# A graph attention layer's rank order and block lists through scatters to memory, and two broadcast rows through transfers

## Chip, cores and metric

One core of one Trainium2 chip. The metric is the device time of one launch in microseconds (us), of which medians are quoted. Ratios are formed only within one submission; where profiles or times of different submissions are set side by side, the text says so. In the profile's lines and in the recorded texts PE is TensorE, DVE is VectorE, ACT is ScalarE, POOL is GpSimd, and SP is the engine whose queue asks for the panels of `adj`; L173 is line 173 of the kernel.

## The reference, cut to what matters

Four graph layers run over the same dense 2708 x 2708 matrix `adj` with 128 features. The change touches layer 1 alone, a graph attention:

```python
XW = X @ W
s_col, s_row = XW @ a[:f], XW @ a[f:]              # called c and r in the kernel
den = exp(leaky_relu(s_row[:, None] + s_col[None, :], 0.01))
num = A @ den
att = where(num != 0, den / num, 0)
H = A @ (att @ XW)
```

The kernel avoids forming `den` densely. It ranks the nodes by c, sorts rows of XW by rank, assigns every node i to one of NB = 43 blocks of ranks (where -r_i falls among the sorted c), and gets `num` from one dense pass (`lc` against all of adj) plus, for each block, a small correction over the at most 128 nodes listed for it. The pass goes through six chunks of columns, four of them 512 wide, by 22 tiles of rows; 16 of these tiles are loaded for each chunk as four panels, the rest stay on the core. These are 132 matmuls in the program. The trace shows each as two records, and the "264 matmuls" of the prediction are records.

Of the kernel before, what the change touches and what calls it, by code (L numbers as in the profile page):

```python
# [8 lines left out]
F32 = mybir.dt.float32  # L9
U32 = mybir.dt.uint32  # L10
I32 = mybir.dt.int32
BF16 = mybir.dt.bfloat16
AF = mybir.ActivationFunctionType
ALU = mybir.AluOpType
AX = mybir.AxisListType

P = 128
# [4 lines left out]
KC = 126  # L22
OOB = 4095
# [27 lines left out]
def kernel(  # L51
# [16 lines left out]
    nc = tc.nc  # L68
    N, D = x.shape
    assert D == P  # L70
    T = (N + P - 1) // P
# [6 lines left out]
    FULL = N // P  # L78
    LAST = N - FULL * P
    NQ = T  # L80
    S = T - RES
    NB = (N + BJ - 1) // BJ
    HALF = N // 2
    pw = [min(P, N - t * P) for t in range(T)]
# [6 lines left out]
    big = ctx.enter_context(tc.tile_pool(name="big", bufs=1))  # L91
# [5 lines left out]
    dram = ctx.enter_context(tc.tile_pool(name="dram", bufs=1, space=bass.MemoryType.DRAM))  # L97
# [4 lines left out]
    def mis_tile():  # L102
        return mis_pool.tile([P, CW], F32, tag="mis", name="mis")
# [19 lines left out]
    ident = const.tile([P, P], F32, tag="ident", name="ident")  # L123
# [18 lines left out]
    def evacuate(n, dst, src):  # L142
        if n % 2:
            nc.scalar.copy(dst, src)
        else:
            nc.vector.tensor_copy(dst, src)
# [70 lines left out]
                op0=ALU.subtract, op1=ALU.mult,  # L217
            )

    def rows_from(dst, col, ts, exp_scale=None):  # L220

        ts = list(ts)
        for g in range(0, len(ts), 4):
            grp = ts[g : g + 4]
            ps = mis_tile()
            w = 0
            for t in grp:
                nc.tensor.transpose(
                    ps[:, w : w + pw[t]], col[: pw[t], t : t + 1].to_broadcast([pw[t], P]), ident[: pw[t], : pw[t]]
                )  # L230
                w += pw[t]
            if exp_scale is None:
                evacuate(g // 4, dst[:, g * P : g * P + w], ps[:, :w])
            else:
                nc.scalar.activation(dst[:, g * P : g * P + w], ps[:, :w], AF.Exp, scale=exp_scale)

    def linear(t, wgt):

        po = mis_tile()
# [11 lines left out]
    e_r = att1.tile([P, T], F32, tag="e_r", name="e_r")  # L251
    f_r = att1.tile([P, T], F32, tag="f_r", name="f_r")
    f_out = att1.tile([P, T], F32, tag="f_out", name="f_out")
    jidx = att1.tile([P, NQ], U32, tag="jidx", name="jidx")
    csort = att1.tile([P, NQ], F32, tag="csort", name="csort")
    g_col = att1.tile([P, NQ], F32, tag="g_col", name="g_col")
    g_inv = att1.tile([P, NQ], F32, tag="g_inv", name="g_inv")
# [299 lines left out]


    wide = ctx.enter_context(tc.tile_pool(name="wide", bufs=1))
    xwe = wide.tile([P, T, D + 1], F32, tag="wide", name="xwe")  # L560
    late = ExitStack()
    got_pool = late.enter_context(tc.tile_pool(name="got", bufs=16))
    sum_pool = late.enter_context(tc.tile_pool(name="sum", bufs=1))
# [31 lines left out]



    xw_rows = dram.tile([N, D], F32, tag="xw_rows", name="xw_rows")
    if LAST:
        nc.gpsimd.memset(xwe[:, FULL, :], 0.0)  # L600
        nc.gpsimd.memset(cc[:, FULL:], 0.0)
# [46 lines left out]
    def times_w(c, t):  # L648
        p, o = pw[t], t * P - starts[c]
        po = mis_tile()  # L650
        nc.tensor.matmul(po[:p, : D + 1], lhsT=xTs[c][:, o : o + p], rhs=wae[:, : D + 1], start=True, stop=True)
        nc.scalar.copy(xwe[:p, t, :], po[:p, : D + 1])

    def compare(t):
        p, o = pw[t], t * P
# [57 lines left out]
        due.flush()  # L713
    late.close()
    lwx = ctx.enter_context(tc.tile_pool(name="lwx", bufs=1))
    xws = lwx.tile([P, NQ, D], F32, tag="xws", name="xws")
    lw = lwx.tile([P, NB, BJ], F32, tag="lw", name="lw")
    g_row = hT

    with tc.tile_pool(name="rank", bufs=1) as rank, tc.tile_pool(name="rank2", bufs=2) as rank2:  # L720
        def rtile(shape, name, dt=F32):
            return rank.tile([P] + shape, dt, tag=name, name=name)

        nc.scalar.dma_start(xw_rows[: FULL * P, :].rearrange("(t p) d -> p t d", p=P), xwe[:, :FULL, :D])
        if LAST:
            nc.scalar.dma_start(xw_rows[FULL * P :, :], xwe[:LAST, FULL, :D])
        nc.vector.tensor_copy(rr, xwe[:, :, D])
        nc.scalar.activation(e_r, rr, AF.Exp)
        nc.scalar.activation(f_r, rr, AF.Exp, scale=0.01)

        rk_f = rtile([T], "rk_f")
        nc.vector.memset(rk_f, float(OOB))
# [2 lines left out]
        nc.vector.tensor_add(rk_f[:, : T - 1], after[:, : T - 1], rows_m[:, : T - 1])  # L735
        lp = pw[T - 1]
        nc.vector.tensor_add(rk_f[:lp, T - 1 :], after[:lp, T - 1 :], rows_m[:lp, T - 1 :])


        grid = [P, T, NB]  # L740
# [46 lines left out]
        nc.vector.tensor_scalar_mul(f_out, f_out, -1.0)  # L787

        place = rtile([T, NB], "place")
        totals = rtile([T, NB], "totals")  # L790
        for t0, t1 in halves:
            rhs = in_b[:, t0:t1, :].rearrange("p t b -> p (t b)")
            for dst, lhs in ((totals, ones_b), (place, upper_b)):
# [10 lines left out]
        nc.vector.tensor_reduce(pos, place, AX.X, ALU.add)  # L804


        val_b = big.tile([P, T, 3, NB], F32, tag="y", name="val_b")
        for n, v in enumerate((node_oob, e_r, f_r)):
            nc.vector.tensor_mul(val_b[:, :, n, :], in_b, v[:, :, None].to_broadcast(grid))
        sl = mis_tile()  # L810
        for t in range(T):
            at = rank2.tile([P, P], F32, tag="at", name="at")
            nc.vector.tensor_scalar(at, iota, pos[:, t : t + 1], None, op0=ALU.is_equal)
            nc.tensor.matmul(
                sl[:, : 3 * NB], lhsT=at, rhs=val_b[:, t, :, :].rearrange("p a b -> p (a b)"),
                start=(t == 0), stop=(t == T - 1),
            )
        for h in range(2):
            nc.vector.tensor_scalar(
                slot_i[h], sl[:, :NB], 2.0, 2.0 * OOB + h, op0=ALU.mult, op1=ALU.add  # L820
            )

        nc.vector.tensor_scalar_add(slot_e, sl[:, NB : 2 * NB], ident[:, KC : KC + 1])
        nc.vector.tensor_scalar_add(slot_f, sl[:, 2 * NB : 3 * NB], ident[:, KC + 1 : KC + 2])


        rk_i = rtile([T], "rk_i", I32)
        nc.vector.tensor_copy(rk_i, rk_f)
        hi_i = rtile([T], "hi_i", I32)
        nc.vector.tensor_single_scalar(hi_i, rk_i, 7, op=ALU.arith_shift_right)  # L830
        hi = rtile([T], "hi")
        nc.vector.tensor_copy(hi, hi_i)
        lo = rtile([T], "lo")
        nc.vector.scalar_tensor_tensor(lo, hi, -float(P), rk_f, op0=ALU.mult, op1=ALU.add)
        of_q = rtile([T, NQ], "of_q")
        nc.vector.tensor_tensor(
            of_q, hi[:, :, None].to_broadcast([P, T, NQ]), iota[:, None, :NQ].to_broadcast([P, T, NQ]),
            op=ALU.is_equal,
        )
        val_q = big.tile([P, T, 2, NQ], F32, tag="y", name="val_q")  # L840
        nc.vector.tensor_mul(val_q[:, :, 0, :], of_q, node[:, :, None].to_broadcast([P, T, NQ]))
        nc.vector.tensor_mul(val_q[:, :, 1, :], of_q, cc[:, :, None].to_broadcast([P, T, NQ]))
        js = mis_tile()
        for t in range(T):
            at = rank2.tile([P, P], F32, tag="at", name="at")
            nc.vector.tensor_scalar(at, iota, lo[:, t : t + 1], None, op0=ALU.is_equal)
            nc.tensor.matmul(
                js[:, : 2 * NQ], lhsT=at, rhs=val_q[:, t, :, :].rearrange("p a q -> p (a q)"),
                start=(t == 0), stop=(t == T - 1),
            )  # L850
        nc.vector.tensor_copy(jidx, js[:, :NQ])
        nc.vector.tensor_copy(csort, js[:, NQ : 2 * NQ])
        nc.scalar.activation(g_col, csort, AF.Exp, scale=0.99)
        nc.scalar.activation(g_inv, csort, AF.Exp, scale=-0.99)
        for q in range(NQ):
            p = pw[q]
            nc.gpsimd.indirect_dma_start(
                out=xws[:p, q, :], out_offset=None, in_=xw_rows[:, :],
                in_offset=bass.IndirectOffsetOnAxis(ap=jidx[:p, q : q + 1], axis=0),
                bounds_check=N - 1, oob_is_err=False,  # L860
            )
            nc.scalar.mul(xws[:p, q, :], xws[:p, q, :], g_col[:p, q : q + 1])
        rows_from(g_row, csort, range(T), 0.99)
        for b in range(NB):
            nc.vector.tensor_scalar(
                lw[:, b, : bw[b]], g_row[:, b * BJ : b * BJ + bw[b]], slot_e[:, b : b + 1], slot_f[:, b : b + 1],
                op0=ALU.mult, op1=ALU.max,
            )

    gb = hT  # L870
    rows_from(gb, rr, range(T), 0.99)
    carry = big.tile([P, N], F32, tag="y", name="carry")

    def mix(w, q, num, col, haccs, pool):

        p = pw[q]
        inv = pool.tile([P, w], F32, tag=f"inv{w}", name="inv")
        nc.scalar.activation(inv[:p], num[:p, :w], AF.Ln)  # L878
        nc.scalar.activation(inv[:p], inv[:p], AF.Exp, scale=-1.0)  # L879

        err = pool.tile([P, w], F32, tag=f"err{w}", name="err")
        nc.vector.tensor_mul(err[:p], inv[:p], num[:p, :w])  # L882
        nc.vector.scalar_tensor_tensor(err[:p], err[:p], 2.0, inv[:p], op0=ALU.subtract, op1=ALU.mult)  # L883
        nc.vector.scalar_tensor_tensor(  # L884
            err[:p], gb[:p, col : col + w], g_inv[:p, q : q + 1], err[:p], op0=ALU.max, op1=ALU.mult
        )
        for o in range(0, w, CW):
            e = min(w, o + CW)
            nc.tensor.matmul(  # L889
                haccs[:, o:e], lhsT=xws[:p, q, :], rhs=err[:p, o:e], start=(q == 0), stop=(q == NQ - 1)  # L890
            )

    def end_carry(c, acc):
# [179 lines left out]
```

## The kernel before: the parts that the change touches

`xwe` holds XW and r; it and `lc` are tiles of one pool with a single buffer.

```python
wide = ctx.enter_context(tc.tile_pool(name="wide", bufs=1))
xwe = wide.tile([P, T, D + 1], F32, tag="wide", name="xwe")
# ... ranks counted (rk_f), blocks found ...
nc.scalar.dma_start(xw_rows[: FULL * P, :].rearrange("(t p) d -> p t d", p=P), xwe[:, :FULL, :D])
lc = wide.tile([P, T, NB, 2], F32, tag="wide", name="lc")   # same buffer as xwe

# block lists: a one-hot compare on VectorE and a matmul on TensorE per tile of nodes
for t in range(T):
    nc.vector.tensor_scalar(at, iota, pos[:, t : t + 1], None, op0=ALU.is_equal)
    nc.tensor.matmul(sl[:, : 3 * NB], lhsT=at, rhs=val_b[:, t, :, :].rearrange("p a b -> p (a b)"),
                     start=(t == 0), stop=(t == T - 1))
# order of ranks: the same with lo/hi of the rank and val_q, giving jidx and csort
# ... cut ...
for q in range(NQ):                        # rows of XW by rank: 22 gathers, each then scaled
    nc.gpsimd.indirect_dma_start(out=xws[:p, q, :], in_=xw_rows[:, :], in_offset=...jidx[:p, q : q + 1]...)
    nc.scalar.mul(xws[:p, q, :], xws[:p, q, :], g_col[:p, q : q + 1])
rows_from(g_row, csort, range(T), 0.99)    # e^.99c on all partitions: 22 turns on TensorE, Exp on ScalarE
rows_from(gb, rr, range(T), 0.99)          # e^.99r: 22 more
carry = big.tile([P, N], F32, tag="y", name="carry")
by_panels(lambda i: lc[: pw[i], i, :, :]..., end_carry)     # the dense pass: 264 records
```

A scheduler orders the instructions of each engine, so the turns and one-hot matmuls above stand inside the pass in TensorE's order. "Turn" means a transpose by a matmul with the identity.

## Time and profile before

| kernel before | us |
|---|---|
| timed, first submission, median of 3 | 1162.3 (1160.76 to 1163.44) |
| the profiled execution | 1204.79 (span 1203.1) |
| last rank count on TensorE ends | 483.05 |
| pass of layer 1 | 490.35 to 634.53 |
| from the ranks to the end of the pass | 151.5 |

The last row is the measure used below: it contains what the change moves up to the end of the pass. What follows the pass took 568.4 to 576.4 us in the 13 profiles (568.6 here, 573.3 in the first profile of the changed kernel and 568.4 in the second), in no order by kernel; differences of some us in the total can lie there. Note at once that the profiled execution is 3.7% slower than the timed ones; what that means becomes clear only in the experiments. The profile's own lines stand in the prediction.

### The profile page before, as it was taken

What the parts mean: (1) busy time and instruction counts of PE and PEld (TensorE: products, weight loads), DVE (VectorE), ACT (ScalarE), POOL (GpSimd) and SP (SyncE); (2) the same over time, 40 slices, a digit from 0 to 9 for tenths busy, and PEclk for the clock granted to TensorE, in tenths of its full rate; (3) what the DMA queues carried; (4) which work ended last, traced back from release to release, by engine and by line L of the source; (5) the groups of instructions that cost most, each with busy time, mean ns of one, the idle gap of its engine ahead of it and who ended that gap; (6) DMA issues with size and microseconds to landing.
All of it is one profiled execution on the core that took longest, in us unless ns stands there. A gap on an engine that the chain in (4) does not pass through costs nothing. (4 is left out here: it accounts for less than half of the span.)

```text
span 1203.1 us, 11015 instructions
## 1 busy us (share of the span) xinstructions
PE 1088.8 (91%) x3625; PEld 515.5 (43%) x3625; DVE 657.8 (55%) x1428; ACT 317.5 (26%) x591; POOL 264.9 (22%) x261
## 2 busy tenths in 40 slices
PE   1899999999946995796799999999899999999997
PEld 1355444443423473253243333333344554465445
DVE  6875469999215476843005999999712112123122
ACT  0001145554001245104005566666311010002000
POOL 4000000001574670007014555565001000000000
PEclk9899999999977896798799999999899999999999
DMA  9994410002715461541653453455375675664754
GB/s 351 372 296 170 141 35 0 1 1 89 269 48 173 150 205 41 176 147 46 202 159 117 149 168 113 128 163 166 109 245 180 191 263 184 209 205 142 250 169 121
DMA packets 113714, 190.88 MB, mean 159 GB/s; under 512 B 13334, under 2 KB 51520, under 8 KB 113652
## 3 DMA queue, kind: packets, MB, share of 16 engines
q1 hardware_dynamic: 90872, 151.05, 38.1%
q0 software_dynamic: 17280, 36.31, 9.6%
q10 hardware_dynamic: 5500, 2.77, 0.8%
q8 instruction: 30, 0.49, 0.2%
q14 instruction: 32, 0.26, 0.1%
HBM read 214.34 MB, written 4.16 MB: 182 GB/s over the span
## 5 line engine op out<-in xcount | busy, mean ns | idle before, releaser
L173 PE MATMUL acc<-part,y 128*128 128x512 f32 (+2 forms) x384 | 160.0, 560 | 0.5 <-issue 0.5
L950 POOL DMA_INDIRECT rows<-in_adjT,slot_i x86 | 122.2, 1421 | 148.6 <-PE num L963 69.5
L963 PE MATMUL num<-rows,lw 128*64 128x512 f32 (+2 forms) x516 | 115.7, 557 | 2.8 <-DMA rows<-in_adjT,slot_i 2.8
L889 PE MATMUL hacc<-err,xws 128*128 128x512 f32 (+3 forms) x264 | 112.4, 562 | 2.2 <-DVE err L884 2.2
L543 PE MATMUL acc<-zT,z 128*128 128x512 f32 (+4 forms) x264 | 107.1, 551 | 0.0
L571 POOL DMA_INDIRECT got<-y_rows,where x88 | 93.3, 1060 | 58.3 <-DVE near_sum L577 21.7
L173 PEld LDWEIGHTS acc<-part,y 128*128 128x128 f32 x384 | 71.2, 196 | 69.0 <-issue 61.9
L173 PE MATMUL acc<-part,lc 128*86 128x512 f32 (+2 forms) x192 | 84.6, 585 | 16.4 <-DMA part<-in_adjT 13.9
L882 DVE TENSOR_TENSOR err<-inv,num 128x1024 f32<-128x1024 f32 (+1 forms) x88 | 74.3, 855 | 22.4 <-ACT inv L879 21.0
L878 ACT ACTIVATE inv<-num 128x1024 f32<-128x1024 f32 (+1 forms) x88 | 64.4, 735 | 83.1 <-PE num L963 79.2
L544 ACT COPY key<-acc 128x512 f32<-128x512 f32 (+3 forms) x132 | 70.2, 534 | 58.2 <-issue 29.8
L374 PE MATMUL acc<-part,y 128*128 128x512 f32 (+2 forms) x192 | 82.3, 581 | 2.2 <-DVE y L197 2.2
L889 PEld LDWEIGHTS hacc<-err,xws 128*128 128x128 f32 (+1 forms) x264 | 46.6, 189 | 79.7 <-issue 40.4
L173 PE MATMUL acc<-part,xs 128*128 128x512 f32 (+2 forms) x192 | 77.9, 546 | 0.1
L884 DVE SCALAR_TENSOR_TENSOR err<-hT,g_inv,err 128x1024 f32<-128x1024 f32 (+1 forms) x88 | 77.1, 917 | 0.0
L173 PE MATMUL acc<-part,mixed 128*128 128x512 f32 (+2 forms) x192 | 75.5, 545 | 0.1
L883 DVE SCALAR_TENSOR_TENSOR err<-err,inv 128x1024 f32<-128x1024 f32 (+1 forms) x88 | 71.8, 857 | 0.0
L184 ACT COPY hT<-acc 128x512 f32<-128x512 f32 (+2 forms) x18 | 9.6, 535 | 230.1 <-PE acc L173 230.1
L543 PEld LDWEIGHTS acc<-zT,z 128*128 128x128 f32 (+1 forms) x264 | 46.8, 186 | 54.0 <-issue 48.7
L545 DVE MAX8 near<-key 128x8 f32<-128x2708 f32 (+1 forms) x22 | 65.4, 2972 | 5.1 <-ACT key L544 5.1
L879 ACT ACTIVATE inv<-inv 128x1024 f32<-128x1024 f32 (+1 forms) x88 | 67.3, 768 | 2.6
L508 POOL TENSOR_TENSOR y<-xs,d2inv 128x2176 f32<-128x2176 f32 (+1 forms) x2 | 4.7, 2325 | 277.4 <-ACT d2inv L506 277.4
(230 smaller groups left out, 1270.9 us busy)
## 6 DMA issues: line engine op xcount, KB each, us to landing
part<-in_adjT SPq DMA_DIRECT2D x102, 1024.0 KB
part<-in_adjT SPq DMA_DIRECT2D x24, 768.0 KB
part<-in_adjT SPq DMA_DIRECT2D x24, 552.0 KB
res<-in_adjT SPq DMA_DIRECT2D x4, 1280.0 KB
got<-y_rows,where POOLq DMA_INDIRECT x88
rows<-in_adjT,slot_i POOLq DMA_INDIRECT x86
rows<-carry SPq DMA_DIRECT2D x86, 10.6 KB
xw_rows<-xwe ACTq DMA_DIRECT2D x1, 1344.0 KB
```

What stands on the lines that cost most here:

```text
L173: nc.tensor.matmul(acc[: lhsT.shape[-1], :w], lhsT=lhsT, rhs=src, start=(i == 0), stop=(i == T - 1 and tick is None))
L374: nc.tensor.matmul(accs[c][:, : cw[c]], lhsT=y[: pw[i], i, :], rhs=src[: pw[i], : cw[c]], start=first, stop=last)
L543: nc.tensor.matmul(pks[c][:p, : cw[c]], lhsT=z2[:, :p], rhs=zT[:, cs], start=False, stop=True)
L544: nc.scalar.copy(key[:p, cs], pks[c][:p, : cw[c]])
L571: nc.gpsimd.indirect_dma_start(out=got[:p, :], out_offset=None, in_=y2_rows[:, :], in_offset=bass.IndirectOffsetOnAxis(ap=where[:p, t, k : ...
L879: nc.scalar.activation(inv[:p], inv[:p], AF.Exp, scale=-1.0)
L882: nc.vector.tensor_mul(err[:p], inv[:p], num[:p, :w])
L883: nc.vector.scalar_tensor_tensor(err[:p], err[:p], 2.0, inv[:p], op0=ALU.subtract, op1=ALU.mult)
L884: nc.vector.scalar_tensor_tensor(err[:p], gb[:p, col : col + w], g_inv[:p, q : q + 1], err[:p], op0=ALU.max, op1=ALU.mult)
L889: nc.tensor.matmul(haccs[:, o:e], lhsT=xws[:p, q, :], rhs=err[:p, o:e], start=(q == 0), stop=(q == NQ - 1))
L950: nc.gpsimd.indirect_dma_start(out=rows[:KC, n, :], out_offset=None, in_=adj_half[:, :], in_offset=bass.IndirectOffsetOnAxis(ap=slot_i[h][ ...
L963: nc.tensor.matmul(num[n * BJ : n * BJ + bw[b], o:e], lhsT=lw[:, b, : bw[b]], rhs=rows[:, n, c0 + o : c0 + e], start=True, stop=True,)
```

## The change

The intent: take the one-hot matmuls, the turns and the row gathers out of TensorE's and VectorE's work by letting GpSimd's indirect transfers put rows where their rank or slot says, and loading them back in order. The two broadcast rows come by writing 22 x 128 values to memory and reading them back to all partitions. The core of the diff:

```diff
-    xwe = wide.tile([P, T, D + 1], F32, tag="wide", name="xwe")
+    xwe = wide.tile([P, T, D + 2], F32, tag="wide", name="xwe")
...
+        nc.vector.tensor_copy(xwe[:, :, D + 1], cc)
+        nc.vector.tensor_copy(rk_u, rk_f)
+        scatter(by_rank, rk_u, xwe)                 # 22 indirect transfers, rows of 520 bytes
...
-        sl, js = one-hot matmuls (44), 22 gathers, 22 scalings on ScalarE   [cut]
+        scatter(by_slot, pos_u, val)                # 22 indirect transfers, rows of 12 bytes
+        on_all(gb, rr, "g_r")
+        nc.gpsimd.dma_start(xws[:, : N // P, :], by_rank[: FULL * P, :].rearrange("(q p) d -> p q d", p=P))
+        nc.gpsimd.dma_start(slots.rearrange("p b v -> p (b v)"), by_slot.rearrange("(p b) v -> p (b v)", p=P))
+        nc.vector.tensor_copy(csort, xws[:, :, D + 1])
+        on_all(g_row, csort, "g_c")
+        nc.gpsimd.tensor_mul(xws[:, :, :D], xws[:, :, :D], g_col[:, :, None].to_broadcast([P, NQ, D]))
-        rows_from(g_row, csort, range(T), 0.99)
-    rows_from(gb, rr, range(T), 0.99)

+        def on_all(dst, col, name):                 # one turn, one Exp, a store and a load
+            nc.tensor.transpose(ps[:T, :P], col, ident)
+            nc.scalar.activation(lines, ps[:T, :P], AF.Exp, scale=0.99)
+            nc.gpsimd.dma_start(flat[:, :], lines)
+            nc.gpsimd.dma_start(dst, <flat, repeated over the partitions>)
```

More of the change, by code (lines that the diff above doesn't have):

```diff
@@ L218, in normalize @@
             )
-    def rows_from(dst, col, ts, exp_scale=None):
-        ts = list(ts)
-        for g in range(0, len(ts), 4):
-            grp = ts[g : g + 4]
-            ps = mis_tile()
-            w = 0
-            for t in grp:
-                nc.tensor.transpose(
-                    ps[:, w : w + pw[t]], col[: pw[t], t : t + 1].to_broadcast([pw[t], P]), ident[: pw[t], : pw[t]]
-                )
-                w += pw[t]
-            if exp_scale is None:
-                evacuate(g // 4, dst[:, g * P : g * P + w], ps[:, :w])
-            else:
-                nc.scalar.activation(dst[:, g * P : g * P + w], ps[:, :w], AF.Exp, scale=exp_scale)
     def linear(t, wgt):
@@ L253 @@
     f_out = att1.tile([P, T], F32, tag="f_out", name="f_out")
-    jidx = att1.tile([P, NQ], U32, tag="jidx", name="jidx")
     csort = att1.tile([P, NQ], F32, tag="csort", name="csort")
@@ L590, in add_near @@
             )
-    xw_rows = dram.tile([N, D], F32, tag="xw_rows", name="xw_rows")
+    by_rank = dram.tile([N, D + 2], F32, tag="by_rank", name="by_rank")
+    by_slot = dram.tile([P * NB, 3], F32, tag="by_slot", name="by_slot")
     if LAST:
@@ L651, in times_w @@
         nc.tensor.matmul(po[:p, : D + 1], lhsT=xTs[c][:, o : o + p], rhs=wae[:, : D + 1], start=True, stop=True)
-        nc.scalar.copy(xwe[:p, t, :], po[:p, : D + 1])
+        nc.scalar.copy(xwe[:p, t, : D + 1], po[:p, : D + 1])
     def compare(t):
@@ L715 @@
     lwx = ctx.enter_context(tc.tile_pool(name="lwx", bufs=1))
-    xws = lwx.tile([P, NQ, D], F32, tag="xws", name="xws")
+    xws = lwx.tile([P, NQ, D + 2], F32, tag="xws", name="xws")
     lw = lwx.tile([P, NB, BJ], F32, tag="lw", name="lw")
-    g_row = hT
-    with tc.tile_pool(name="rank", bufs=1) as rank, tc.tile_pool(name="rank2", bufs=2) as rank2:
+    gb = hT
+    with tc.tile_pool(name="rank", bufs=1) as rank:
         def rtile(shape, name, dt=F32):
             return rank.tile([P] + shape, dt, tag=name, name=name)
-        nc.scalar.dma_start(xw_rows[: FULL * P, :].rearrange("(t p) d -> p t d", p=P), xwe[:, :FULL, :D])
-        if LAST:
-            nc.scalar.dma_start(xw_rows[FULL * P :, :], xwe[:LAST, FULL, :D])
         nc.vector.tensor_copy(rr, xwe[:, :, D])
@@ L729, with scatter @@
         nc.scalar.activation(f_r, rr, AF.Exp, scale=0.01)
+        def on_all(dst, col, name):
+            ps = mis_tile()
+            nc.tensor.transpose(ps[:T, :P], col, ident)
+            lines = rank.tile([T, P], F32, tag=name, name=name)
+            nc.scalar.activation(lines, ps[:T, :P], AF.Exp, scale=0.99)
+            flat = dram.tile([T, P], F32, tag=name + "_d", name=name + "_d")
+            nc.gpsimd.dma_start(flat[:, :], lines)
+            nc.gpsimd.dma_start(dst, bass.AP(tensor=flat.tensor, offset=flat.offset, ap=[[0, P], [1, N]]))
+        def scatter(out, idx, src):
+            for t in range(T):
+                p = pw[t]
+                ins = nc.gpsimd.indirect_dma_start(
+                    out=out[:, :], out_offset=bass.IndirectOffsetOnAxis(ap=idx[:p, t : t + 1], axis=0),
+                    in_=src[:p, t, :], in_offset=None, bounds_check=out.shape[0] - 1, oob_is_err=False,
+                )
+                tc.declare_no_dep(ins.ins, group=out.name, reason="rows of a permutation")
+                tc.add_to_no_dep_group(out.name, ins.ins)
+        zeros = rtile([3 * NB], "zeros")
+        nc.gpsimd.memset(zeros, 0.0)
+        nc.gpsimd.dma_start(by_slot.rearrange("(p b) v -> p (b v)", p=P), zeros)
+        nc.gpsimd.memset(xws[:, NQ - 1, :], 0.0)
+        nc.vector.tensor_copy(xwe[:, :, D + 1], cc)
         rk_f = rtile([T], "rk_f")
@@ L737 @@
         nc.vector.tensor_add(rk_f[:lp, T - 1 :], after[:lp, T - 1 :], rows_m[:lp, T - 1 :])
+        rk_u = rtile([T], "rk_u", U32)
+        nc.vector.tensor_copy(rk_u, rk_f)
+        scatter(by_rank, rk_u, xwe)
         grid = [P, T, NB]
@@ L789 @@
         place = rtile([T, NB], "place")
-        totals = rtile([T, NB], "totals")
+        totals = rank.tile([P, T, NB], F32, tag="first", name="totals")
         for t0, t1 in halves:
@@ L804 @@
         nc.vector.tensor_reduce(pos, place, AX.X, ALU.add)
-        val_b = big.tile([P, T, 3, NB], F32, tag="y", name="val_b")
+        val = rtile([T, 3], "val")
         for n, v in enumerate((node_oob, e_r, f_r)):
-            nc.vector.tensor_mul(val_b[:, :, n, :], in_b, v[:, :, None].to_broadcast(grid))
-        sl = mis_tile()
-        for t in range(T):
-            at = rank2.tile([P, P], F32, tag="at", name="at")
-            nc.vector.tensor_scalar(at, iota, pos[:, t : t + 1], None, op0=ALU.is_equal)
-            nc.tensor.matmul(
-                sl[:, : 3 * NB], lhsT=at, rhs=val_b[:, t, :, :].rearrange("p a b -> p (a b)"),
-                start=(t == 0), stop=(t == T - 1),
-            )
+            nc.vector.tensor_copy(val[:, :, n], v)
@@ new lines @@
+        nc.vector.scalar_tensor_tensor(pos, pos, float(NB), blk, op0=ALU.mult, op1=ALU.add)
+        pos_u = rtile([T], "pos_u", U32)
+        nc.vector.tensor_copy(pos_u, pos)
+        scatter(by_slot, pos_u, val)
+        on_all(gb, rr, "g_r")
+        nc.gpsimd.dma_start(
+            xws[:, : N // P, :], by_rank[: FULL * P, :].rearrange("(q p) d -> p q d", p=P)
+        )
+        if LAST:
+            nc.gpsimd.dma_start(xws[:LAST, FULL, :], by_rank[FULL * P :, :])
+        slots = rtile([NB, 3], "slots")
@@ L818 @@
+        nc.gpsimd.dma_start(slots.rearrange("p b v -> p (b v)"), by_slot.rearrange("(p b) v -> p (b v)", p=P))
         for h in range(2):
             nc.vector.tensor_scalar(
-                slot_i[h], sl[:, :NB], 2.0, 2.0 * OOB + h, op0=ALU.mult, op1=ALU.add
+                slot_i[h], slots[:, :, 0], 2.0, 2.0 * OOB + h, op0=ALU.mult, op1=ALU.add
             )
-        nc.vector.tensor_scalar_add(slot_e, sl[:, NB : 2 * NB], ident[:, KC : KC + 1])
-        nc.vector.tensor_scalar_add(slot_f, sl[:, 2 * NB : 3 * NB], ident[:, KC + 1 : KC + 2])
@@ L827 @@
-        rk_i = rtile([T], "rk_i", I32)
-        nc.vector.tensor_copy(rk_i, rk_f)
-        hi_i = rtile([T], "hi_i", I32)
-        nc.vector.tensor_single_scalar(hi_i, rk_i, 7, op=ALU.arith_shift_right)
-        hi = rtile([T], "hi")
-        nc.vector.tensor_copy(hi, hi_i)
-        lo = rtile([T], "lo")
-        nc.vector.scalar_tensor_tensor(lo, hi, -float(P), rk_f, op0=ALU.mult, op1=ALU.add)
-        of_q = rtile([T, NQ], "of_q")
-        nc.vector.tensor_tensor(
-            of_q, hi[:, :, None].to_broadcast([P, T, NQ]), iota[:, None, :NQ].to_broadcast([P, T, NQ]),
-            op=ALU.is_equal,
-        )
@@ L840 @@
-        val_q = big.tile([P, T, 2, NQ], F32, tag="y", name="val_q")
-        nc.vector.tensor_mul(val_q[:, :, 0, :], of_q, node[:, :, None].to_broadcast([P, T, NQ]))
-        nc.vector.tensor_mul(val_q[:, :, 1, :], of_q, cc[:, :, None].to_broadcast([P, T, NQ]))
-        js = mis_tile()
-        for t in range(T):
-            at = rank2.tile([P, P], F32, tag="at", name="at")
-            nc.vector.tensor_scalar(at, iota, lo[:, t : t + 1], None, op0=ALU.is_equal)
-            nc.tensor.matmul(
-                js[:, : 2 * NQ], lhsT=at, rhs=val_q[:, t, :, :].rearrange("p a q -> p (a q)"),
-                start=(t == 0), stop=(t == T - 1),
-            )
@@ L851 @@
-        nc.vector.tensor_copy(jidx, js[:, :NQ])
-        nc.vector.tensor_copy(csort, js[:, NQ : 2 * NQ])
+        nc.vector.tensor_scalar_add(slot_e, slots[:, :, 1], ident[:, KC : KC + 1])
+        nc.vector.tensor_scalar_add(slot_f, slots[:, :, 2], ident[:, KC + 1 : KC + 2])
+        nc.vector.tensor_copy(csort, xws[:, :, D + 1])
         nc.scalar.activation(g_col, csort, AF.Exp, scale=0.99)
         nc.scalar.activation(g_inv, csort, AF.Exp, scale=-0.99)
-        for q in range(NQ):
-            p = pw[q]
-            nc.gpsimd.indirect_dma_start(
-                out=xws[:p, q, :], out_offset=None, in_=xw_rows[:, :],
-                in_offset=bass.IndirectOffsetOnAxis(ap=jidx[:p, q : q + 1], axis=0),
-                bounds_check=N - 1, oob_is_err=False,
-            )
-            nc.scalar.mul(xws[:p, q, :], xws[:p, q, :], g_col[:p, q : q + 1])
@@ L863 @@
-        rows_from(g_row, csort, range(T), 0.99)
+        g_row = rtile([N], "g_row")
+        on_all(g_row, csort, "g_c")
+        nc.gpsimd.tensor_mul(xws[:, :, :D], xws[:, :, :D], g_col[:, :, None].to_broadcast([P, NQ, D]))
         for b in range(NB):
@@ L868 @@
             )
-    gb = hT
-    rows_from(gb, rr, range(T), 0.99)
     carry = big.tile([P, N], F32, tag="y", name="carry")
@@ L889, in mix @@
             nc.tensor.matmul(
-                haccs[:, o:e], lhsT=xws[:p, q, :], rhs=err[:p, o:e], start=(q == 0), stop=(q == NQ - 1)
+                haccs[:, o:e], lhsT=xws[:p, q, :D], rhs=err[:p, o:e], start=(q == 0), stop=(q == NQ - 1)
             )
```

## The prediction

> **What bounds the kernel now.** I read the page first (PE is busy 91% of the span, so TensorE time is the currency), then the chain that ended last (PE nearly throughout, one line of matmuls, L173, 25%), then the timeline of each engine between 480 and 640 us, the stretch that the change rewrites: the preparation of layer 1 and its dense pass of 264 matmuls over all of adj ("lc" against "part" and "res"). Last came the waits of the SP queue.
>
> ```profile
> PE 1088.8 (91%) x3625; PEld 515.5 (43%) x3625; DVE 657.8 (55%) x1428; ACT 317.5 (26%) x591; POOL 264.9 (22%) x261
> ...
> 489.21 0.34 DVE L776 TENSOR_TENSOR lc<-sel,e_r 128x172 f32<-128x172 bf16 x1
> ...
> 490.35 5.09 PE L173 MATMUL acc<-part,lc 128*86 128x512 f32 x6 [2.48 <-DVE lc L776]
> ...
> 521.67 0.61 PE L814 MATMUL mis<-val_b,at 128*128 128x129 f32 x4
> 522.11 1.02 PE L173 MATMUL acc<-part,lc 128*86 128x512 f32 x2
> 522.97 0.61 PE L814 MATMUL mis<-val_b,at 128*128 128x129 f32 x4
> ...
> 541.48 2.66 PE L228 MATMUL mis<-ident,csort 128*128 128x128 f32 x22
> 544.07 0.65 PE L228 MATMUL mis<-ident,rr 128*128 128x128 f32 x4
> ...
> 556.19 8.05 PE L173 MATMUL acc<-part,lc 128*86 128x512 f32 x18
> 577.88 6.55 PE L173 MATMUL acc<-part,lc 128*86 128x512 f32 x8 [13.64 <-DMA part<-in_adjT]
> ...
> 631.42 3.11 PE L173 MATMUL acc<-res,lc 128*86 128x276 f32 x12
> ```
>
> The reader is to see where the pass begins (1.1 us after the first piece of lc exists), where it ends (634.5), and what stands inside it. It takes 144.2 us. Undisturbed it would take 101.7: the same shapes in the last three layers take 19.27 us for 512 columns (44 records), 14.22 for 384 and about 10.4 for 276, and there are four, one and one. The overhead of 42.5 us is:
> - L814, the one-hot turns of the slot lists: a cycle of 1.30 us holds two records of the pass (0.876) and four of L814, so 0.43 us, eleven times: 4.7 us.
> - L847, the same for ranks: cycles of 1.27 us, 0.39 x 11 = 4.3 us.
> - L228 on csort: 541.48 to 544.07, 2.6 us.
> - L228 on rr: 544.07 to 556.19, in which only six records of the pass (2.6 us) are done: 9.5 us. PE waits there for ScalarE, whose evacuations queue behind the scaling of xws, paced by the gathers.
> - The stop at 563.9 to 577.9 for a panel of adj, and the half clock after it (6.55 us for 8 records in place of 3.5): 16.6 us.
> - Start at half clock, prefix counts, a short last wait: 4.8 us.
>
> ```profile
> 541.51 1.01 POOL L857 DMA_INDIRECT xws<-xw_rows,jidx  x1 [89.40 <-DVE carry L146]
> ...
> 569.04 0.95 POOL L857 DMA_INDIRECT xws<-xw_rows,jidx  x1 [0.30 <-issue]
> ...
> 544.10 0.40 ACT L862 ACTIVATE xws<-xws,g_col 128x128 f32<-128x128 f32 x1 [0.36 <-DMA xws<-xw_rows,jidx]
> ...
> SPq L151 <- remote: 38.6, 1, 38.6
> ```
>
> GpSimd issues 22 indirect transfers at a pitch of (569.04 - 541.51) / 21 = 1.31 us; the first is usable 2.6 us after its start. The last line is the queue of SP: it waited 38.6 us, until 572.7, to ask for the next panel. The buffer was free from about 557 on by PE's own records; PE's semaphore updates arrived up to 16 us late while the 22 gathers ran back to back. This stop may belong to the profiled run: that run took 1204.8 us, the three timed ones 1162. A similar lateness stands around 331 to 366 us. I give 60% that timed runs have little of it.
>
> **What the Trainium skill says.** (1) "DMA: Bandwidth & Descriptors", section "Anatomy of one DMA — SWDGE (gpsimd) path": such a transfer has a fixed cost of about 2.0 us, mostly the receipt of the last write, plus bytes over 436 GB/s. The 2.6 us above (1.0 of it issue) agree. (2) "Perfetto Trace Analysis", section "DMA Instruction — SWDGE (GPSIMD)": the end shown is that of descriptor generation, not of the data. So the 1.0 us per gather is not when its source or target is free; the trace agrees (end at 542.5, use at 544.1). (3) "TensorE: Matmul & The Clock Gate", Part 1: an idle window of about 3.4 us halves the clock. The trace agrees in kind: records of 592 ns became 1057 ns after the waits near 550.
>
> **The change part by part.** I compared the order of instructions on each engine of both built programs.
>
> Removed: L814, L847 and both L228 groups: 4.7 + 4.3 + 2.6 + 9.5 = 21.1 us, all inside the pass, so on the path. The one-hot compares (44 at 286 ns) and value grids leave DVE, and 22 scalings leave ScalarE; those lie beside PE and buy nothing by themselves. The 22 gathers go; the one store of xw_rows from the ACT queue goes.
>
> Added: 22 scatters of 520-byte rows to memory, 22 of 12-byte rows, five loads or stores around them, all on GpSimd's queue, and two small turns on PE (0.3 us).
>
> The point that I think decides: lc and xwe share one buffer (the pool "wide" has a single one). Before, the only late readers of xwe were a store issued at 479.9 and 482.5, gone by about 488 (its packets end there), so lc was written at 489.21 without a wait. After, xwe is read by the 22 scatters, and in DVE's order the first write of lc waits for all eight semaphores of GpSimd's transfers, that is for the last scatter. The ranks are ready at 483.6; with a cast and the zero fill ahead on GpSimd the first scatter starts at about 485. The last starts at 485 + 21 x 1.31 = 512.5 and lands 2.6 us later, at 515.1. lc is thus 25.9 us late, PE starts the pass at about 516.2, and its idle time before the pass, at 483 to 490 now, grows by as much. Nothing else can fill it: the three panels are loaded, and the rest of PE's order is behind lc.
>
> Second: the turn of csort stands in PE's order after seven of the first 22 matmuls, and csort now comes from the load of xws back from memory, which waits for the scatters. PE gets there at about 525 to 526 (2.5 us of half clock, the prefix counts, seven at 0.876). The load is 1.40 MB: issue at 515, 2.0 + 3.2 us by the skill's formula (an estimate), 1 to 3 us for issuing 2688 rows, so 520 to 523; the copy of csort stands in DVE's order behind all of lc, 11.2 us after its first piece, 526.3. I put 3 us for this wait, 1 for the second prefix count, 2 for the half clock that a wait brings.
>
> Then GpSimd scales xws (4.7 us, as L508's two instructions over the same 2816 columns together), and scatters the slots from about 535 to 564; slots land at about 569, the row of e^.99c at 574, lw (9.7 us on DVE) at 584. The pass ends far later, so this whole second half is hidden.
>
> Sum: + 25.9 + 0.3 + 3 + 1 + 2 - 21.1 = + 11 us, if the stop for a panel is the same in both. The layers after it are untouched.
>
> **The rivals.** (a) The gain of the turns is what remains: lc isn't held, because the scatters are quicker than gathers or start earlier. For it: 20 us of PE work really go. Against: the wait stands in the built order, and a gather with 20 rows cost 0.95 us against 1.0 with 128, so the pitch is a fixed cost. It would give 1162 - 20 = 1142. (b) The stop at 564 to 578 is real in timed runs and goes with the gathers: then + 11 - 16.6 = - 6, 1156. Against: 22 back-to-back scatters at 535 to 564, also inside the pass, are the same pattern and may stop SP in the same way; then 1173. (c) Scatters are dearer: 1.42 us was the mean of L950's indirect transfers while DVE was busy, against 1.00 for L857. At a pitch of 1.7 lc comes 8 us later still; a slow generation of 2688 row descriptors adds up to 10 us at the csort turn: 1182 to 1191. (d) The second chain through GpSimd outlasts the pass. It has over 35 us of room, so I give this 5%.
>
> **Range and chances.** Base sum 1173. The stop vanishing while it was real before (15%, - 16.6) pulls it down by 2.5, and (a) in part by another 2; (c) pushes up by about 1. I say 1169, with 1150 (between (a) and (b)) to 1187 (the middle of (c)). Faster by 2% needs under 1139, which not even (a) reaches: 4%. Slower by 2% needs over 1185: 13%. Within 2%: 83%.
>
> **What would show it.** Right: the first lc on DVE ended by a wait for the scatters at about 515, DVE and PE idle from 488 to 516, PE's idle before the lc group at about 25 us and not 2.5; the pass then close to 110 us and not 144 (with a stop, 120 to 127), ending about 626; a wait at the seventh matmul for csort; the slots and lw done 30 us and more before the end of the pass. Wrong: lc written at 489 as before; or scatters at another pitch than 1.3 us; or the row gathers of L950 starting late because slot_i or lw is; or the span before the preparation or after the pass changed by more than 5 us.

## The result, and the profile after

The changed kernel takes 1169.07 us (1168.31 to 1169.29, four runs), the kernel before in the same submission 1162.1 (four runs). The ratio is 1.0059, 95% interval 1.0041 to 1.0076: within 2%. A ratio here is the mean time of one kernel's fast runs over that of the other's of the same rounds, so not quite the ratio of the medians.

First, VectorE's timeline of the changed kernel (start, busy us, engine, line, operation; in brackets the idle time before and what ended it):

```profile
485.96 0.34 DVE L788 TENSOR_TENSOR lc<-sel,e_r 128x172 f32<-128x172 bf16 x1 [25.98 <-DMA by_rank<-xwe,rk_u]
...
497.11 0.23 DVE L843 COPY csort<-xws 128x22 f32<-128x22 f32 x1 [1.78 <-DMA xws<-by_rank]
...
549.71 9.65 DVE L850 TENSOR_SCALAR lw<-g_row,slot_e,slot_f 128x64 f32<-128x64 f32 x43 [6.43 <-DMA g_row<-g_c_d]
```

The first piece of `lc` waits 25.98 us for the scatters that read `xwe`, the tile in whose buffer it is written. Before, the same instruction had no bracket at all. `lw`, the last product of the second chain, ends at 559.4.

GpSimd's timeline of the changed kernel shows why the wait is that long:

```profile
455.63 1.98 POOL L726 DMA_INDIRECT by_rank<-xwe,rk_u  x1 [0.30 <-DVE first L754]
457.91 0.98 POOL L726 DMA_INDIRECT by_rank<-xwe,rk_u  x1 [0.30 <-issue]
...
483.66 0.94 POOL L726 DMA_INDIRECT by_rank<-xwe,rk_u  x1 [0.31 <-issue]
488.57 1.50 POOL L828 DMA_DIRECT2D xws<-by_rank  x1 [3.98 <-issue]
...
536.49 0.92 POOL L726 DMA_INDIRECT by_slot<-val,pos_u  x1 [0.31 <-issue]
```

From the second to the last scatter by rank there are 20 pitches in 25.75 us: 1.29 us each, although a row tile of 128 x 520 bytes is small. The last lands 2.3 us after its start, at 485.96, when `lc` starts.

TensorE's timeline of the changed kernel:

```profile
487.10 2.01 PE L173 MATMUL acc<-part,lc 128*86 128x512 f32 x2 [28.42 <-DVE lc L788]
...
497.49 0.27 PE L715 MATMUL mis<-ident,csort 128*22 128x128 f32 x1
497.59 7.89 PE L173 MATMUL acc<-part,lc 128*86 128x512 f32 x18
...
590.80 3.11 PE L173 MATMUL acc<-res,lc 128*86 128x276 f32 x12
```

TensorE idles 28.42 us ahead of the pass. The pass then runs from 487.10 to 593.91, 106.8 us instead of 144.2, with neither a wait for csort nor a stop for a panel. From the ranks (453.72) to its end: 140.2 us, 11.3 less than in the profile of before. Yet the timed runs say 7 us more. The two profiles cannot be subtracted: everything ahead of the ranks, which the change does not touch, is 29.3 us earlier in the changed kernel's profile (453.72 against 483.05). This shows in layer 0. Here is ScalarE's timeline there, before:

```profile
349.43 0.58 ACT L698 COPY hT<-acc 128x512 f32<-128x512 f32 x1 [47.45 <-remote]
```

and after:

```profile
334.08 0.59 ACT L682 COPY hT<-acc 128x512 f32<-128x512 f32 x1 [32.19 <-PE acc L570]
```

That copy follows a small matmul. TensorE's timeline before:

```profile
332.80 0.49 PE L588 MATMUL acc<-ident,near_sum 128*128 128x128 f32 x2 [0.51 <-DVE near_sum L579]
```

It ended at 333.3, so ScalarE seems to have learnt of it some 16 us late (the bracket of its copy says "remote" and names no instruction). In the changed kernel the same pair (333.55 and 334.08) is 0.04 us apart. GpSimd issues layer 0's gathers in this stretch. So the experiments had three questions: does the `lc` wait give back the work removed, do the stops belong to one execution, a chip or a kernel, and what does the change do to them?

### The profile page after: what moved, and what is told of

It is laid out like the page before. It is cut to its first block, busy times and chain, and to the rows that moved or that the text cites. A ratio compares the mean times of both kernels' runs of the same rounds, so it can differ in the third digit from the quotient of the medians.

```text
span 1167.2 us, 10739 instructions
## 1 busy us (share of the span) xinstructions
PE 1063.9 (91%) x3495; PEld 497.2 (43%) x3495; DVE 647.2 (55%) x1380; ACT 304.2 (26%) x559; POOL 294.6 (25%) x294
## 5 line engine op out<-in xcount | busy, mean ns | idle before, releaser
L933 POOL DMA_INDIRECT rows<-in_adjT,slot_i x86 | 118.1, 1373 | 143.5 <-PE num L946 85.0
L173 PE MATMUL acc<-part,lc 128*86 128x512 f32 (+2 forms) x192 | 77.3, 558 | 28.6 <-DVE lc L788 28.4
L553 POOL DMA_INDIRECT got<-y_rows,where x88 | 93.5, 1062 | 35.4 <-issue 10.7
## 6 DMA issues: line engine op xcount, KB each, us to landing
rows<-carry SPq DMA_DIRECT2D x86, 10.6 KB
```

The source lines that it names most:

```text
L173: nc.tensor.matmul(acc[: lhsT.shape[-1], :w], lhsT=lhsT, rhs=src, start=(i == 0), stop=(i == T - 1 and tick is None))
L553: nc.gpsimd.indirect_dma_start(out=got[:p, :], out_offset=None, in_=y2_rows[:, :], in_offset=bass.IndirectOffsetOnAxis(ap=where[:p, t, k : ...
L933: nc.gpsimd.indirect_dma_start(out=rows[:KC, n, :], out_offset=None, in_=adj_half[:, :], in_offset=bass.IndirectOffsetOnAxis(ap=slot_i[h][ ...
```

## The experiments

Eleven runs in three submissions, on the chips numbered 15, 0 and 10 (no number is on record for the first submission). In all three the kernel before takes 1209 us, not 1162, in 15 or 16 runs each. I call this the slow kind. The first submission's kind did not come again.

| run (chip) | us, median | ratio to before | ranks to end of pass, us | stop for a panel of the 512-column chunks, us |
|---|---|---|---|---|
| before, profiled (15) | 1210.43 | 1.000 | 151.7 | 13.4 |
| before, profiled (0) | 1209.0, one run | | 150.7 | 13.9 |
| before, profiled (10) | 1206.32, one run | | 149.8 | 13.3 |
| changed, first submission | 1169.07 | 1.006 | 140.2 | none |
| changed (0) | 1210.98 | 0.999 | 150.8 | 8.7 |
| lc moved (15) | 1196.50 | 0.987 | 136.4 | none |
| lc moved, csort later (15) | 1176.92 | 0.973 | 115.2 | 1.6 |
| same (0) | 1176.29 | 0.971 | 117.8 | 3.1 |
| same (10) | 1174.12 | 0.972 | 115.8 | 0.9 |
| rows alone (15) | 1192.95 | 0.985 | 134.9 | 10.3 |
| scatters added, unused (0) | 1237.20 | 1.020 | 173.0 | 11.5 |
| changed, slots spaced (10) | 1197.38 | 0.991 | 140.2 | none |

Differences in the fourth column explain those in time: rows alone is 16.8 us shorter there and 16.4 in time than before on its chip; the added scatters 22.3 longer and 28 in time (24 by the ratio); slots spaced 9.6 shorter and 11 in time. By the rule of 2%, with 95% intervals, only the three runs with `lc` moved and csort later are faster; the added scatters are "unclear" (1.015 to 1.025), and all others are within 2%.

### The kernel before again, three profiles

No edit.

> The kernel before, unchanged, profiled once more. Question: does the stop for a panel in the pass of layer 1 (563.9 to 577.9 us) and the stretch of late semaphore updates near 331 to 366 us belong to the kernel or to the one profiled execution, which took 1204.8 us where the timed ones took 1162? If it belongs to that execution: profiled span near 1160, no wait of 13.6 us for a panel of adj, the pass of layer 1 at 144.2 - 16.6 = 127 us. If it belongs to the kernel: profiled span again near 1200, pass near 144. Time 1162 in both.

> The kernel before, one profile on this chip, to have the pass of layer 1 of both kernels on the same chip. Fast chip: no stop of 13 us for a panel in the pass (127 us long), no late updates at 331 to 366 us, span near 1160. Slow chip: both again, span 1205 to 1210.

> The kernel before, one profile, again for a chip of the fast kind: pass of layer 1 about 127 us with no stop for a panel, no 30 us in layer 0's gathers, span near 1160. On a slow chip 1205 to 1210 with both stops.

All three show both stops. TensorE's timeline of the kernel before on chip 0:

```profile
484.49 0.71 PE L680 MATMUL rk<-ones_b,mask 20*128 20x1 bf16 x21 [2.53 <-DVE mask L659]
...
492.50 4.55 PE L173 MATMUL acc<-part,lc 128*86 128x512 f32 x6 [2.47 <-DVE lc L776]
...
579.48 6.29 PE L173 MATMUL acc<-part,lc 128*86 128x512 f32 x8 [13.89 <-DMA part<-in_adjT]
```

So the stops are not an accident of one execution: they come wherever before takes 1209 us. My first profile of before had come from that kind, while its timing had not. A profile of before on the fast kind was not to be had; that it has no stop there rests on the sum: about 30 us in layer 0 and 16.6 in the pass make the 47 between 1209 and 1162. Whether the chip or something else set for a whole submission makes the kind is open.

### Rows alone

The kernel before, with only the two broadcast rows taken from the change:

```diff
-        rows_from(g_row, csort, range(T), 0.99)
+        on_all(g_row, csort, "g_c")
-    rows_from(gb, rr, range(T), 0.99)
+    on_all(gb, rr, "g_r")
```

> The kernel before with one part of the change alone: the rows of e^.99r and e^.99c come through memory (one turn of the columns, one exponential of 22 x 128, a store and a load repeated over the partitions) and not by 44 turns on PE; gathers, one-hot turns and buffers stay. By my sum 2.6 (turns of csort) and 9.5 (turns of rr, where PE waits for ScalarE's evacuations) leave the pass: 1162 - 12 = 1150, ratio 0.990. If those 9.5 us were only PE standing beside another limit (the panel of adj that comes next): 1159 to 1162.

The pass is 127.6 us long instead of 144.4 on the same chip. TensorE's timeline:

```profile
543.52 0.28 PE L223 MATMUL mis<-ident,csort 128*22 128x128 f32 x1
543.64 0.27 PE L223 MATMUL mis<-ident,rr 128*22 128x128 f32 x1
543.75 13.90 PE L173 MATMUL acc<-part,lc 128*86 128x512 f32 x32
...
583.66 5.07 PE L173 MATMUL acc<-part,lc 128*86 128x512 f32 x8 [10.25 <-DMA part<-in_adjT]
```

Of the 16.8 us, 4.8 are the shorter stop (10.25 idle and 5.07 for eight records, against 13.43 and 6.68). The other 12.0 are the turns: I had put them at 2.6 + 9.5. They were real work on the path, and the transfers in their place cost nothing that shows.

### The suspected cost alone: scatters added, unused

The kernel before with the 22 scatters by rank, whose result nobody reads. TensorE's order is unchanged.

```diff
+        rk_u = rtile([T], "rk_u", U32)
+        nc.vector.tensor_copy(rk_u, rk_f)
+        for t in range(T):
+            nc.gpsimd.indirect_dma_start(out=by_rank[:, :], out_offset=...rk_u[:p, t : t + 1]...,
+                                         in_=xwe[:p, t, :], ...)
```

> The kernel before, with the 22 scatters of the rows of xwe by rank added and used by nobody; all turns and gathers stay, and the order on PE is unchanged. It adds the one suspected cost alone. Theory 1 (lc waits for the buffer that the scatters read, DVE and PE stand for 26 us): first lc ended by a wait of about 26 us, the pass begins 26 us later, time + 23 to + 28 us, ratio 1.020 to 1.024. Rival 2 (the scatters do no harm, the loss of the change lies elsewhere): within 5 us of before. The 22 gathers start later but behind the turns of val_q as before, so the stop for a panel stays where the chip has it.

VectorE's timeline of this kernel:

```profile
517.10 0.34 DVE L788 TENSOR_TENSOR lc<-sel,e_r 128x172 f32<-128x172 bf16 x1 [24.72 <-DMA by_rank<-xwe,rk_u]
```

The pass starts 32.4 us after the ranks in place of 7.3: 25.1 later, and the ratio is 1.020 (24 us). The scatters by themselves cost what the theory says, and the trace shows it at this wait. The rival, that they do no harm, has fallen.

### lc moved to another buffer

The changed kernel, with `lc` in the other large buffer and the later large tiles exchanged so that no space is added. The run's output was checked and correct.

```diff
-        lc = wide.tile([P, T, NB, 2], F32, tag="wide", name="lc")
+        lc = big.tile([P, T, NB, 2], F32, tag="y", name="lc")
-    carry = big.tile([P, N], F32, tag="y", name="carry")
+    carry = wide.tile([P, N], F32, tag="wide", name="carry")
```

> The changed kernel, with lc moved from the single buffer it shares with xwe to the other large buffer (and the later large tiles exchanged between the two, so that no space is added). Theory 1 (lc waits 26 us for the 22 scatters that read xwe, and that gives back the turns removed) together with the second wait I see in the built order: lc is written near 461 us instead of 486 and the pass starts near 461, but PE's turn of csort stands after 15 matmuls of the pass and csort still comes near 497, so PE is held there for about 20 us; net gain 6 to 7 us, 1162 us. Theory 1 without that second wait (lc is all): 1169 - 26 = 1143. Rival 2 (the turns removed were never worth 21 us, or transfers slow the pass): the pass starts early but becomes longer by as much with matmuls slowed rather than held: 1165 to 1171, with no wait for csort over 10 us.

TensorE's timeline, and VectorE's copy of csort:

```profile
497.25 3.62 PE L173 MATMUL acc<-part,lc 128*86 128x512 f32 x4 [2.47 <-DVE lc L788]
...
534.87 0.37 PE L715 MATMUL mis<-ident,csort 128*22 128x128 f32 x1 [21.93 <-DVE pos L823]
534.55 0.18 DVE L843 COPY csort<-xws 128x22 f32<-128x22 f32 x1 [21.42 <-DMA xws<-by_rank]
```

The pass starts 7.4 us after the ranks, as before the change, and then TensorE is held 21.93 us at the turn of csort. The bracket names VectorE's `pos`, but that instruction started at 534.64, just after csort's copy; what VectorE itself waited for is the last line: 21.42 us, until the load `xws<-by_rank`, started at 525.86, had landed. 26 less 22 is 4 us; the whole gain of 14.4 us over the changed kernel (136.4 against 150.8 on another chip of the slow kind) contains in addition the stop for a panel, about 10 us, which this kernel does not have. I had expected 6 to 7 and had not foreseen that.

### lc moved and csort's users later

In addition everything that depends on csort is placed behind the second chunk of the pass:

```diff
-        nc.vector.tensor_copy(csort, xws[:, :, D + 1])
-        on_all(g_row, csort, "g_c")            # and g_col, g_inv, the scaling of xws, lw
+        def by_ranks(): ...                     # the same instructions
+        # in end_carry(c, acc), when c == 1:
+            with tc.issue_after(mm), tc.issue_after(copied[0]):
+                by_ranks()
```

> As the run with lc moved to the other large buffer, and in addition everything that depends on csort (its copy, the exponentials, the turn on PE, the scaling of xws, lw) placed in the order of the engines after the second chunk of the pass. Theory 1: both waits are off PE; the pass starts near 461 us, runs about 107 us without a stop and ends near 568 (594 in the changed kernel); time 1169 - 26 = 1143, ratio to the kernel before 0.983. Rival 2 (removed turns were worth little, or the scatters' transfers slow the pass): pass of 120 us or more beside the scatters, time 1155 to 1169. Rival 3 (something later, the row of e^.99c or lw, sets the end of the pass): mix starts late by a wait for GpSimd's work, 1150 to 1160.

> The version with lc in the other large buffer and csort's users after the second chunk, once more, beside the changed kernel on one chip. Slow chip: 1177 again, 22 to 26 us under the changed kernel. Fast chip: 1143 to 1146, ratio 0.984 to before, again 23 to 26 us under the changed kernel. If the gain of the first run (0.973) was mostly the slow chip's stop: ratio above 0.99 on a fast chip.

> The version with lc in the other buffer and csort's users after the second chunk a third time, for a chip of the fast kind: there 1143 to 1146 us, ratio 0.984 to before. On a slow one 0.971 to 0.973 as before, and then it tells nothing new.

TensorE's timeline on chip 0:

```profile
490.93 3.42 PE L173 MATMUL acc<-part,lc 128*86 128x512 f32 x4 [2.47 <-DVE lc L788]
...
531.82 0.27 PE L715 MATMUL mis<-ident,csort 128*22 128x128 f32 x1
...
564.65 5.36 PE L173 MATMUL acc<-part,lc 128*86 128x512 f32 x8 [3.06 <-DMA part<-in_adjT]
```

Both waits are gone. From the ranks to the end of the pass it takes 117.8 us against 150.8 for the changed kernel on the same chip; the 33 us are 26 of the `lc` wait and some 5 of the stop (10.2 us of idle and slowed records there, 4.9 here); of the remaining 2, 1.6 are a wait of the changed kernel at the turn of csort (shown in the next experiment). The ratio to before is 0.971 to 0.973 on three chips, so this version beats the kernel before there by over 2%, and the changed kernel too on chip 0, where both ran (1176.29 against 1210.98 us). It was not run on the fast kind, where my expectation of 1143 stays open. An estimate from these numbers: before without its stop needs 151.5 - 16.6 = 134.9 us, this version 115.2 to 117.8, so some 17 to 20 us less than 1162.

### The changed kernel on the slow kind

No edit.

> The changed kernel, unchanged, beside the kernel before on whatever chip this is. The chip of the first four runs gives the kernel before 1209 us and that of the first timing 1162. The profiles of before on the slow chip show two stops that I take for the difference: about 30 us in the gathers of layer 0 (331 to 366 us), which the change doesn't touch, and 13 to 17 us for a panel of adj in the pass of layer 1, which it does. If that is so: on a slow chip the stop in layer 0 is there in the changed kernel too, that in the pass is not (no 22 gathers with back-to-back late updates), and the time is 1209 + 7 - 16 = 1200, ratio 0.993; on a fast chip 1169 again, ratio 1.006. If the ratio belongs to the kernels and not to the chip: 1.006 on both, 1216 on a slow one.

The ratio is 0.9988 (0.9957 to 1.0019), and the expected 0.993 fails. TensorE's timeline on chip 0:

```profile
517.13 2.00 PE L173 MATMUL acc<-part,lc 128*86 128x512 f32 x2 [28.41 <-DVE lc L788]
...
527.81 0.27 PE L715 MATMUL mis<-ident,csort 128*22 128x128 f32 x1 [1.59 <-DVE totals L810]
...
560.25 10.53 PE L173 MATMUL acc<-part,lc 128*86 128x512 f32 x24
579.43 5.03 PE L173 MATMUL acc<-part,lc 128*86 128x512 f32 x8 [8.65 <-DMA part<-in_adjT]
...
631.48 3.11 PE L173 MATMUL acc<-res,lc 128*86 128x276 f32 x12
```

The `lc` wait is the same to 0.01 us as in the first submission, but the changed kernel has a stop for a panel too. It costs 10.7 us: the pass takes 117.5 here and 106.8 there. I had thought that the stop goes with the gathers; there is one while the scatters of the slots run. TensorE also waits 1.59 us at the turn of csort, where it did not wait in the first submission. The transfers' rate in 40 slices of 540 to 590 us, same run:

```profile
GB/s 99 315 322 114 44 151 247 396 387 388 194 239 383 327 351 259 17 1 1 1 1 1 0 9 122 269 286 303 284 400 408 398 387 390 378 61 69 339 393 38
```

From 560 to 570 us (the slices at 17, 1, ... 9) almost nothing moves: the panel is late because it is asked for late, not for lack of bandwidth. SP's own record says how late. In the undisturbed profile SP asks for the four panels of a chunk 3.7, 7.1, 10.6 and 14.0 us after the chunk begins (chunk at 510.72, requests at 514.4 to 524.7). Here the scatters of the slots run from 539.97 to 567.90. The chunk that begins at 541.04 is still served on this schedule (requests at 544.7 to 555.0). The first request of the chunk that begins at 560.25 is due at 564.0 and comes at 571.0.

### The changed kernel with the slots' scatters spaced

Two dummy fills on GpSimd between each two of the 22 scatters of the slots:

```diff
                 tc.add_to_no_dep_group(out.name, ins.ins)
+                if spaced:
+                    nc.gpsimd.memset(idle, 0.0)     # 128 x 600, twice
+                    nc.gpsimd.memset(idle, 0.0)
...
-        scatter(by_slot, pos_u, val)
+        with tc.manual_schedule(engines={nc.gpsimd.engine}):
+            scatter(by_slot, pos_u, val, spaced=True)
```

> The changed kernel with the 22 scatters of the slots spaced: two dummy fills of a 600 column tile by GpSimd stand between each two, so their pitch goes from 1.28 to about 2.4 us; all else stays. On a chip where before takes 1209 us, the changed kernel's pass still had a stop for a panel (8.65 us, then half clock), while these scatters ran back to back. Theory: the back-to-back indirect transfers of GpSimd hold up PE's semaphore updates that the SP queue waits for on such a chip; spaced they do not: no stop over 3 us in the pass, time 8 to 10 us less than the changed kernel, ratio to before about 0.991 in place of 0.999. Rival (the panel is late for another reason, such as the bandwidth or PE's own progress): the stop stays, 0.999. On a chip where before takes 1162 us there was no stop: 1169 again, ratio 1.006. The slots come about 25 us later and stay hidden by some 5 to 10 us in all cases.

GpSimd's timeline, then TensorE's:

```profile
549.79 0.61 POOL L735 MEMSET idle<- 128x600 f32 x1
550.46 0.60 POOL L736 MEMSET idle<- 128x600 f32 x1
551.22 0.98 POOL L728 DMA_INDIRECT by_slot<-val,pos_u  x1 [0.16 <-issue]
```

```profile
560.74 13.97 PE L173 MATMUL acc<-part,lc 128*86 128x512 f32 x32
574.54 5.47 PE L173 MATMUL acc<-res,lc 128*86 128x512 f32 x12
...
621.47 3.11 PE L173 MATMUL acc<-res,lc 128*86 128x276 f32 x12
```

At a pitch of 2.4 us the stop is gone and the pass takes 106.8 us, as in the first submission. The ratio is 0.991 in place of 0.999, as expected (0.989 to 0.993 against 0.996 to 1.002, on two chips of the slow kind). GpSimd now does more work and the kernel is 10 us faster by these ratios. So on the slow kind running the scatters back to back is part of what makes the stop. The edit changed one thing more: the store and the load of the row e^.99c now stand among the first scatters (542.04 and 547.41); before they followed the last, at 567.89 and 569.89.

Back-to-back scatters alone are not enough, however. The kernel with `lc` moved ran the same 22 scatters back to back inside the pass, on the slow kind too. GpSimd's timeline there:

```profile
535.47 1.06 POOL L726 DMA_INDIRECT by_slot<-val,pos_u  x1 [0.30 <-DVE pos_u L825]
...
562.38 0.92 POOL L726 DMA_INDIRECT by_slot<-val,pos_u  x1 [0.31 <-issue]
```

The requests of its chunk from 542.87 on came on schedule at 546.6, 550.0 and 553.4, the fourth 1.8 us late at 558.7, and TensorE did not stop. In the kernel before, the late request was due 15 us after the first gather, and in the changed kernel 24 us after the first scatter; requests due earlier than that were on time. But the fourth request here was due 21 us after the first scatter and came only 1.8 us late, so the place in the series does not settle it either. How the transfers hold up a request is not shown: late news of TensorE's progress, as in layer 0, fits, and layer 0's own stop was not tested.

## Why the prediction was right or wrong

The total was right: 1169 predicted, 1169.07 measured. The mechanism that decides was right too; that the number was met to a tenth is luck, because inside it terms too large were set against pulls that did not happen.

- **The wait for the shared buffer: right.** 25.9 us predicted, 25.98 measured and 25.97 on the slow kind. Taking it away (with the next wait) gains 33 us on one chip, of which 26 are this wait, and adding it alone costs 24.
- **The work removed: right as far as tested.** 12.1 of the 21.1 us are the turns; the run of rows alone gives 12.0. The 9.0 of the one-hot matmuls were not tested alone.
- **The terms around csort: wrong in size.** I added 3 us for a wait at its turn, 1 for the second prefix count, 2 for the half clock that a wait brings, and 0.3 for new turns. The pass would then have taken 101.7 + 4.8 + 6.3 = 112.8 us; it took 106.8. These 6.3 us were really 0.3 in that profile. The 3 us did not follow from my own times either: TensorE there at 525 to 526 and csort at 526.3 make a wait of about 1 us. Csort came when I said, 11.2 us after the first `lc`, but TensorE came no earlier: after its long idle the granted clock was 0.50 until 490 us and 0.69 from there to 495 (eight records in 5.16 us where full speed takes 3.5), so its turn followed at 497.49, just after csort. On the slow kind the clock came back sooner (0.92 in the five us from 520, the eight records in 3.98 us), and TensorE did wait for csort, 1.59 us there and 1.28 with the slots spaced. In these three profiles the wait is there where the clock returned sooner; a half clock after it shows in none. With 25.9 and -21.1 this leaves +5.1; from the ranks to the end of the pass, kernels without stops differ by 140.2 - 134.9 = +5.3, and the timed difference is +7. The 134.9 is an estimate (151.5 less the stop of 16.6), as no profile of before on the fast kind exists; the rest of 1.7 us was not traced.
- **The stop for a panel: right that timed runs might lack it, wrong about what it belongs to.** I gave 60% that it was one profiled execution's. It was in every profile of before, all of the slow kind, and absent from the only profile of the fast kind, which is the changed kernel's. Rivals (a) and (b) had pulled the base sum of 1173 down to 1169; neither was what made up for the oversized terms around csort.
- **Rival (b), second half: right in kind, on the slow kind only.** A panel is late there while the scatters of the slots run, and costs 10.7 us against 16.6 before. So the same change is +5.3 - 16.6 + 10.7, about zero: the measured 0.999.
- **Rivals (a), (c), (d): not so.** The pitch was 1.29, not 1.7, the issue of the load of `xws` took 1.50 us, and the second chain ended 34 us before the pass.

## What to carry to other kernels

Before work is moved from an engine to transfers, look at which tile the transfers read and who is next to write its buffer: here a shared buffer turned 22 small scatters at 1.29 us each into 26 us on the path, and took back all that the change had saved on the kind of chip that it was first timed on. A wait taken away may uncover the next one in the engine's order (26 us became 22 at csort), so both have to be moved. And check that a profile and the timings come from the same kind of run before its gaps are priced.

## What the Trainium skill lacked or had wrong

- "DMA: Bandwidth & Descriptors", section "Anatomy of one DMA — SWDGE (gpsimd) path", gives about 2.0 us plus bytes over 436 GB/s. A scatter agrees (2.3 us from start to use). The load of `xws`, 1.40 MB in rows of 520 bytes, should take 5.2 us by it (an estimate) and took 8.5 from the start of its issue (488.57 to 497.11), of which issue was 1.50. From 494.3 on a panel of `adj` was loaded beside it, so how much of the excess belongs to the rows is not shown.
- "Perfetto Trace Analysis", section "DMA Instruction — SWDGE (GPSIMD)", is right that the end shown is that of descriptor generation (a scatter shown as ended at 484.60 was still waited for until 485.96), but neither page gives the pitch at which GpSimd starts such transfers one after another: 1.28 to 1.29 us, the same for rows of 520 and of 12 bytes.
- No page that I read has the following: where before takes 1209 us and not 1162, a request for a panel that falls due during a series of back-to-back indirect transfers of GpSimd can come late (7 us in the changed kernel, with a stop of 8.65 us), and a pitch of 2.4 us removed this stop. The stops of 13.3 to 13.9 us in the kernel before and ScalarE's copy that came 16 us late in layer 0 stand beside such transfers too; their cause was not tested.
